# In the fourth layer of a graph network: half the pair-adds in every other chunk, the normalized rows in a buffer of their own, and GAT outputs and last operations two slots later

## The chip, the core and the metric

The kernel runs on one core of a Trainium2 chip. A core has five engines that run their own instruction queues in order and meet only at semaphores: TensorE (PE in the profile; its weight loads are PEld), VectorE (DVE), ScalarE (ACT), GpSimd (POOL) and SyncE (SP). DMAs are issued from queues of SP, ACT and POOL. The metric is the time of one execution on the device in microseconds; lower is better.

## What is computed

Four graph layers on 8 batches of 2048 nodes with 128 features, one shared 0/1 adjacency matrix. About 16 of 2048 entries of a row are set. Layers 0 and 1 are masked attention blocks with 8 heads and a feed-forward part. Layers 2 and 3 are GAT layers, and the change concerns these:

```python
def _L3_gnn_ref(x, adj, W, a_src, a_dst, ln_gamma, ln_beta):
...
    h = x @ W
    s_i = h @ a_src
    s_j = h @ a_dst
    e = s_i[:, :, None] + s_j[:, None, :]
    e = jnp.where(e >= 0, e, NEG_SLOPE * e)
    e = jnp.where(adj[None, :, :] == 0, -jnp.inf, e)
    att = jax.nn.softmax(e, axis=-1)
    att = jnp.nan_to_num(att, nan=0.0)
    out = jnp.einsum('bij,bjd->bid', att, h)
    y = out + x
    mu = jnp.mean(y, axis=-1, keepdims=True)
    var = jnp.mean((y - mu) ** 2, axis=-1, keepdims=True)
    return ln_gamma * (y - mu) * jax.lax.rsqrt(var + LN_EPS) + ln_beta
```

## The kernel before

**Tiles and chunks.** Nodes are sorted by their number of neighbours and cut into 16 tiles of 128 nodes, one node to a partition. Tile t has CAPS[t] slots, from 30 in tile 0 down to 11 in tile 15: slot s of a partition holds the s-th neighbour of that node. In a GAT layer the slots of a tile are cut into chunks of 4 or 3 (75 chunks with 277 slots in a layer). A chunk variable `k` is the first slot of the chunk in its tile. For each slot one indirect DMA (`gather`, line 320, queue of POOL) brings the row of the neighbour from the table of the layer in DRAM: 8 batches x 128 features and 2 x 8 weights, 1040 float32, 128 rows at a time. Chunks land in six buffers `kv0` to `kv5` that are used in turn; the gathers of a chunk wait until TensorE has read the chunk six before.

**What a GAT chunk does** (`gat_chunk`, a generator whose four parts are emitted at different times):

- Part A, lines 753 to 759: VectorE works out the weights of the slots by small products and maxima. They go to the PSUM tile `pair`, and those of two batches to the SBUF tile `ws`.
- Part B, lines 765 to 770: VectorE multiplies the rows of six batches by their weights (128x3072 for four slots), ScalarE those of the other two (two ACTIVATEs of 128x128 per slot).
- Part C, lines 772 to 774: VectorE adds the upper slots of the chunk to the lower ones in place, so of 4 slots 2 are left (an add of 128x2048), and of 3 also 2 (128x1024).
- Part D, lines 778 to 784: TensorE multiplies what is left by the identity and so sums it in the PSUM accumulator `acc`, two matmuls of 128x512 for each slot that is left. `acc` has two buffers, one per tile in work.

**What a tile does at its end.** `sums` (line 463 to 470) makes the reciprocals of the sums of weights. `tail` (line 1138) lets some slots pass and then emits `outputs` (line 657): `o = acc * sums` on VectorE, the only reader of `acc`. Then `gat_tail` starts a slot later: TensorE adds the residual and the bias (`added`, lines 801 to 810, PSUM tiles `m`), ScalarE squares with a sum (`squares`, line 817), GpSimd takes the power -1/2 (line 844, tile `rs`; it stands in the same queue as the gathers), three slots pass, ScalarE scales (`scaled`, line 825). In layer 2 each half is then transposed, projected to the table row of layer 3, and put into the table by an indirect DMA of GpSimd (`put_rows`, line 502); in layer 3 three slots pass, VectorE multiplies by gamma and adds beta (lines 858 and 860), and an indirect DMA of GpSimd writes the result (line 862). In layer 3 squares, scaled rows and result are held in the tile `rows`, of which there is one buffer.

**The order of the work** is written out by hand. `layers` goes over the chunks of all layers. For chunk i of a GAT layer it emits, in this order: `fetch` (the gathers of chunks up to four ahead); part A of chunk i; a slot; part B of chunk i; a slot; parts C and D of chunk i-1; a slot. A slot advances every waiting generator by one step, first `threads` (there a `tail` counts its slots), then `tails` (there a `gat_tail` makes one step). So a chunk is three slots long. Layer 3's first gathers are emitted once tiles 0 to 12 of layer 2 are put; the first chunks of layer 3 are those of tiles 0 and 1, in the order of `ORDER[4]`, with gathers from `sorted_lists`.

Of the kernel before, what the change touches and what calls it, by code (L numbers as in the profile page):

```python
# [8 lines left out]
F32 = mybir.dt.float32  # L9
# [8 lines left out]
P = 128  # L18
B, N, D = 8, 2048, 128
NT = N // P  # L20
NH = 8
# [7 lines left out]
NB = 8  # L29
# [8 lines left out]
CAPS = [BASE + FOLD, 23, 21, 20, 19, 18, 18, 17, 16, 16, 15, 14, 14, 13, 12, 11]  # L38
# [44 lines left out]
def sparse_path(ctx: ExitStack, tc: tile.TileContext, ins: dict, out: bass.AP, flag: bass.AP):  # L83
# [10 lines left out]
    nc = tc.nc  # L94
    const = ctx.enter_context(tc.tile_pool(name="const", bufs=1))
    work = ctx.enter_context(tc.tile_pool(name="work", bufs=2))
# [6 lines left out]
    def misc():  # L103
        return pm.tile([P, 512], F32, tag="m", name="m")
# [221 lines left out]
    def transpose4(src):  # L326
        pt = misc()
        for j in range(4):
            nc.tensor.transpose(pt[:, j * P : (j + 1) * P], src[:, j, :], ident)  # L329
        return pt.rearrange("p (b c) -> p b c", c=P)  # L330
# [111 lines left out]
    def folded_sums(w, box):  # L442

        columns = w.shape[-1]
        ps = misc()[:, :columns]
        for i in range(FOLD):
            nc.tensor.matmul(ps, merge, w[:, i, :], start=i == 0, stop=i == FOLD - 1)
        box["folded"] = small.tile([P, columns], F32, tag="folded", name="folded", bufs=1)
        nc.scalar.copy(box["folded"], ps)
# [107 lines left out]
    def state_done(l, t, box):  # L557


        box["halves"] = box.get("halves", 0) + 1  # L560
        if box["halves"] == 2:
            if l < 3:
                nc.sync.dma_start(kept[t], box["x"].rearrange("p b n -> p (b n)"))
                put_rows(l + 1, t, box["rows"])
                put[l + 1] += 1
            state(l, t + 3)
# [95 lines left out]
    def rows_of(box):  # L662
        if "rows" not in box:
            box["rows"] = work.tile([P, NB * 2 * D], F32, tag="rows", name="rows", bufs=1)
        return box["rows"]
# [70 lines left out]
    def gat_chunk(l, c):  # L736
        box, t, k, ns = c["box"], c["t"], c["k"], c["ns"]
        mine = own[:, t, :]
        if c["folded"]:
            pf = misc()[:, :NB]  # L740
            nc.tensor.matmul(pf, spread, mine, start=True, stop=True)
            mine = small.tile([P, NB], F32, tag="mine", name="mine", bufs=1)
            nc.scalar.copy(mine, pf)
            yield
        if k == 0:
            box["acc"] = pacc.tile([P, NB // 4, 512], F32, tag="acc", name="acc")
            at, n = (0 if t % 2 == 0 else 512 - NB * CAPS[t]), CAPS[t]
            box["w"] = pair[:, at : at + NB * n].rearrange("p (s b) -> p s b", b=NB)
        acc, w = box["acc"], box["w"]
        hs = c["buf"]  # L750
        wc = w[:, k : k + ns, :]
        wa, wb = hs[:, :, NB * D : NB * (D + 1)], hs[:, :, NB * (D + 1) :]
        nc.vector.tensor_mul(wb, wb, mine[:, None, :].to_broadcast([P, ns, NB]))
        nc.vector.tensor_max(wc, wa, wb)
        if c["folded"]:
            box["wf"] = small.tile([P, FOLD, NB], F32, tag="wf", name="wf", bufs=1)
            nc.vector.tensor_max(box["wf"], wa, wb)
        ws = small.tile([P, 4, SCALED], F32, tag="ws", name="ws", bufs=3)
        nc.vector.tensor_max(  # L759
            ws[:, :ns, :], wa[:, :, NB - SCALED :], wb[:, :, NB - SCALED :]  # L760
        )
        yield
        hv = hs[:, :, : NB * D].rearrange("p s (b c) -> p s b c", b=NB)
        nv = NB - SCALED
        nc.vector.tensor_mul(  # L765
            hv[:, :, :nv, :], hv[:, :, :nv, :], wc[:, :, :nv, None].to_broadcast([P, ns, nv, D])
        )
        for i in range(ns):
            for b in range(nv, NB):
                nc.scalar.mul(hv[:, i, b, :], hv[:, i, b, :], ws[:, i, b - nv : b - nv + 1])  # L770
        yield
        left = -(-ns // 2)
        if ns > 1:
            nc.vector.tensor_add(hv[:, : ns - left], hv[:, : ns - left], hv[:, left:ns])  # L774
        yield
        if c["folded"]:
            folded_sums(box["wf"], box)
        for i in range(left):
            for j in range(NB // 4):
                nc.tensor.matmul(  # L780
                    acc[:, j, :], merge if c["folded"] else ident, hv[:, i, 4 * j : 4 * j + 4, :],
                    start=k + i == 0, stop=c["last"] and i == left - 1,
                )
        yield

    def gat_tail(l, t, box):

        wt = W[l]
        xT = box["x"]
        if l == 2:  # L790
            ns = [work.tile([P, 4, D], F32, tag="n", name="n2") for _ in range(2)]
        else:
            n = rows_of(box)[:, : B * D].rearrange("p (b d) -> p b d", d=D)
            ns = [n[:, :4, :], n[:, 4:, :]]
        ys = [None, None]
        ss = small.tile([P, 8], F32, tag="ss", name="ss", bufs=3)
        rs = small.tile([P, 8], F32, tag="rs", name="rs", bufs=3)

        def added(h):
            ys[h] = y = misc().rearrange("p (b c) -> p b c", c=D)  # L800
            nc.tensor.matmul(
                y, ones_bf, wt["row_z"][:, None, :].to_broadcast([P, 4, D]),
                start=True, stop=False, skip_group_check=True,
            )
            nc.tensor.matmul(
                y, ident, box["o"][:, 4 * h : 4 * h + 4, :], start=False, stop=False,
                skip_group_check=True,
            )
            for j in range(4):
                nc.tensor.matmul(  # L810
                    y[:, j, :], xT[:, 4 * h + j, :], wt["res1"], start=False, stop=True,
                    skip_group_check=True,
                )

        def squares(h):
            for j in range(4):
                nc.scalar.activation(
                    ns[h][:, j, :], ys[h][:, j, :], AF.Square, bias=eps, scale=D**-0.5,
                    accum_out=ss[:, 4 * h + j : 4 * h + j + 1],
                )  # L820

        def scaled(h):
            for j in range(4):
                at = 4 * h + j
                nc.scalar.mul(ns[h][:, j, :], ys[h][:, j, :], rs[:, at : at + 1])  # L825

        def half_rows(h):
            scaled(h)
            yield
            pt = transpose4(ns[h])  # L830
            yield
            nc.scalar.copy(xT[:, 4 * h : 4 * h + 4, :], pt)
            yield
            yield from project(3, 4 * h, xT, rows_of(box), t)
            yield
            state_done(l, t, box)

        added(0)
        yield
        squares(0)  # L840
        added(1)
        yield
        squares(1)
        nc.gpsimd.tensor_tensor(rs, ss, half, op=ALU.pow)
        for _ in range(3):
            yield
        if l == 2:
            parts = [half_rows(0), later(2, lambda: half_rows(1))]
            while parts:
                advance(parts)  # L850
                yield
        else:
            scaled(0)
            yield
            scaled(1)
            for _ in range(3):
                yield
            nc.vector.tensor_mul(n, n, last_g[:, None, :].to_broadcast([P, B, D]))
            yield
            nc.vector.tensor_add(n, n, last_b[:, None, :].to_broadcast([P, B, D]))  # L860
            yield
            nc.gpsimd.indirect_dma_start(
                out=out, out_offset=bass.IndirectOffsetOnAxis(ap=perm[:, t : t + 1], axis=0),
                in_=n.rearrange("p b d -> p (b d)"), in_offset=None,
            )
            state_done(l, t, box)
            state_done(l, t, box)
# [213 lines left out]
    for l in range(4):  # L1081
        per = 2 if l < 2 else 4
        for t, k, ns, folded in pieces(l, per):
            c = dict(l=l, t=t, k=k, ns=ns, folded=folded, box=blocks[l][t])
# [48 lines left out]
    def later(n, make):  # L1133
        for _ in range(n):
            yield
        yield from make()

    def tail(l, t, box):
        for _ in range(2 if l < 2 else 3):
            yield  # L1140
        outputs(l, t, box)
        if l < 2:
            tails.append(later(1, lambda: attention_tail(l, t, box, 0)))
            tails.append(later(4, lambda: attention_tail(l, t, box, 4)))
        else:
            tails.append(later(1, lambda: gat_tail(l, t, box)))
        yield
# [600 lines left out]
```

## Time and profile before

| | us |
|---|---|
| median of 3 runs | 3423.61 (3417.87 to 3426.96) |
| the profiled execution | 3428.05 |
| its span | 3426.3 |
| layers 0 and 1, about | 353 to 2224 of the span |
| layer 2, steady part | 2360 to 2760 |
| from layer 2 to layer 3 | 2760 to 2890 |
| layer 3, from the last put to the last gather | 2890 to 3370 |
| end | 3370 to 3427 |

In the lines below, "busy" is the time in which an engine worked on an instruction; "x" is a count; "idle before us" is how long the engine stood still just before instructions of the group, and after the arrow stands what ended most of that. In a table of windows the columns are the stretch, its length, and for each engine its busy time with the number of instructions, then the granted clock of TensorE as a share of full speed, the mean busy share of the 16 DMA engines and the rate. A timeline line gives start, length, engine, line, operation, output and input.

### The profile page before, as it was taken

The numbers are of one execution on the slowest core, as the hardware profiler recorded it, in microseconds if no ns is written. First come the engines' busy times: TensorE is split into PE (matmuls) and PEld (weight loads), VectorE is DVE, ScalarE is ACT, GpSimd is POOL, SyncE is SP. The second block draws the span as 40 slices with busy tenths as digits, with TensorE's granted clock in tenths as the row PEclk, the third lists the DMA queues.
The fourth block names the chain that finished last, engine by engine and source line by source line (L and its number), as shares of the span: only waits on it lengthen the run. The fifth ranks groups of instructions, "written<-read, shape, count | busy, mean of one in ns | idle before, by whom it ended". The sixth has DMA issues, their size and how long they took to land.

```text
span 3426.3 us, 34767 instructions
## 1 busy us (share of the span) xinstructions
PE 2761.3 (81%) x10618; PEld 1595.4 (47%) x10618; DVE 3051.6 (89%) x2807; ACT 1425.1 (42%) x4972; POOL 2229.1 (65%) x1453
## 2 busy tenths in 40 slices
PE   5657888788899996888889899976888986767775
PEld 4523445455555652545455555553444543333332
DVE  8799999999999989999999999947867866889885
ACT  4712333334344441333334344453545654445444
POOL 0065888687667654566677666637767865788773
PEclk9888999999999999999999999998988998888887
DMA  8697778888878777677888888658988986899873
GB/s 326 201 355 275 284 283 303 307 303 301 312 290 296 277 287 280 238 309 284 335 298 292 315 297 295 241 171 307 326 290 311 352 326 214 291 313 334 304 275 118
DMA packets 200625, 986.52 MB, mean 288 GB/s; under 512 B 31918, under 2 KB 33712, under 8 KB 128436
## 3 DMA queue, kind: packets, MB, share of 16 engines
q0 software_dynamic: 175024, 890.45, 72.2%
q1 hardware_dynamic: 20502, 75.52, 5.9%
q10 hardware_dynamic: 4904, 18.24, 1.7%
q8 instruction: 87, 1.43, 0.2%
q14 instruction: 108, 0.88, 0.1%
HBM read 937.16 MB, written 91.55 MB: 300 GB/s over the span
## 4 chain that ended last, share of the span: by engine, by line
DVE 36%; PE 23%; issue 19%; DMA 11%; POOL 4%; ACT 4%; POOLq 0%; ACTq 0%; DVEq 0%; another core or an unknown queue 0%
DVE kv L614 13%; DVE kv L628 13%; PE acc L780 7%; PE acc L638 5%; DMA kv<-table,lists 4%; POOL kv L320 3%; DVE sc L617 3%; DMA kv<-table,sorted_lists 2%; DVE kv L774 2%; PE m L329 2%; DVE kv L765 2%; DMA table<-rows,perm 1%; DMA xs<-in_x_nodes_dram,perm 1%; PE m L720 1%; DVE w L459 1%
## 5 line engine op out<-in xcount | busy, mean ns | idle before, releaser
L320 POOL DMA_INDIRECT kv<-table,lists x955 | 1463.0, 1532 | 381.6 <-issue 203.6
L638 PE MATMUL acc<-kv,ident 128*128 128x512 f32 x2200 | 1109.0, 634 | 221.8 <-DVE kv L628 221.3
L780 PE MATMUL acc<-kv,ident 128*128 128x512 f32 x1184 | 622.2, 679 | 190.9 <-DVE kv L774 157.7
L638 PEld LDWEIGHTS acc<-kv,ident 128*128 128x128 f32 x2200 | 413.1, 201 | 652.7 <-issue 365.9
L617 DVE TENSOR_REDUCE sc<-kv 128x128 f32<-128x2048 f32 (+1 forms) x284 | 634.0, 2233 | 9.2
L628 DVE TENSOR_TENSOR kv<-kv,w 128x2048 f32<-128x2048 f32 (+1 forms) x284 | 631.5, 2223 | 8.6 <-ACT w L623 7.9
L614 DVE TENSOR_TENSOR kv<-kv,q 128x2048 f32<-128x2048 f32 (+1 forms) x282 | 629.2, 2231 | 10.7 <-DMA kv<-table,sorted_lists 5.7
L780 PEld LDWEIGHTS acc<-kv,ident 128*128 128x128 f32 x1184 | 248.9, 220 | 514.4 <-issue 294.8
L765 DVE TENSOR_TENSOR kv<-kv,pair 128x3072 f32<-128x3072 f32 (+1 forms) x150 | 466.2, 3108 | 1.0
L484 POOL TENSOR_TENSOR rs<-ss,half 128x4 f32<-128x4 f32 x128 | 222.8, 1741 | 313.9 <-ACT n L479 313.0
L774 DVE TENSOR_TENSOR kv<-kv 128x2048 f32<-128x2048 f32 (+1 forms) x150 | 296.1, 1974 | 145.9 <-ACT kv L770 137.0
L770 ACT ACTIVATE kv<-kv,ws 128x128 f32<-128x128 f32 x1108 | 339.0, 406 | 175.2 <-DVE ws L759 108.9
L479 ACT ACTIVATE n<-m,eps 128x128 f32<-128x128 f32 x512 | 181.0, 366 | 423.6 <-PE m L720 212.5
L623 ACT ACTIVATE w<-sc,lmask 128x64 f32<-128x64 f32 x554 | 165.1, 352 | 443.8 <-DVE sc L617 425.5
L320 POOL DMA_INDIRECT kv<-table,sorted_lists x153 | 203.5, 1330 | 114.8 <-PE acc L638 45.9
L488 ACT ACTIVATE n<-m,rs 128x128 f32<-128x128 f32 x512 | 146.0, 370 | 124.4 <-POOL rs L484 124.2
L502 POOL DMA_INDIRECT table<-rows,perm x57 | 102.5, 1798 | 129.1 <-ACT rows L553 33.2
L329 PE MATMUL m<-ident,n 128*128 128x128 f32 x640 | 105.2, 287 | 67.3 <-ACT n L825 47.4
L720 PE MATMUL m<-w_L_w,hT 128*128 128x128 f32 x1024 | 156.6, 275 | 1.7 <-ACT hT L704 1.7
L329 PEld LDWEIGHTS m<-ident,n 128*128 128x128 f32 x640 | 82.4, 147 | 132.6 <-ACT n L825 57.6
L720 PEld LDWEIGHTS m<-w_L_w,hT 128*128 128x128 f32 x1024 | 135.2, 192 | 1.9 <-ACT hT L704 1.9
L699 PE MATMUL m<-n1T,w_L_gnn_W 128*128 128x512 f32 x256 | 131.6, 597 | 0.8 <-ACT n1T L694 0.4
(242 smaller groups left out, 3476.4 us busy)
## 6 DMA issues: line engine op xcount, KB each, us to landing
kept<-xT SPq DMA_DIRECT2D x48, 512.0 KB
xT<-kept SPq DMA_DIRECT2D x48, 512.0 KB
kv<-in_adj_dram SPq DMA_DIRECT2D x16, 1024.0 KB
table<-kv ACTq DMA_DIRECT2D x16, 1024.0 KB
kv<-table,lists POOLq DMA_INDIRECT x955
kv<-in_x_nodes_dram SPq DMA_DIRECT2D x16, 512.0 KB
kv<-table,sorted_lists POOLq DMA_INDIRECT x153
found<-cand POOLq DMA_DIRECT2D x16, 64.0 KB
```

What stands on the lines that cost most here:

```text
L320: nc.gpsimd.indirect_dma_start(out=dst, out_offset=None, in_=tables[l][:, :], in_offset=bass.IndirectOffsetOnAxis(ap=index, axis=0), bound ...
L329: nc.tensor.transpose(pt[:, j * P : (j + 1) * P], src[:, j, :], ident)
L484: nc.gpsimd.tensor_tensor(rs, ss, half[:, :4], op=ALU.pow)
L614: nc.vector.tensor_mul(kk, kk, q[:, None].to_broadcast([P, ns, NB, D]))
L617: nc.vector.tensor_reduce(sc[:, :ns].rearrange("p s (b h) -> p (s b) h", h=NH), kk.rearrange("p s b (h j) -> p (s b) h j", h=NH), axis=AX. ...
L628: nc.vector.tensor_mul(vv, vv, w[:, k : k + ns, :].rearrange("p s (b h) -> p (s b) h", h=NH)[:, :, None, :] .to_broadcast([P, ns * NB, HD, ...
L638: nc.tensor.matmul(acc[:, j, :], merge if c["folded"] else ident, kv[:, i, 4 * j : 4 * j + 4, D:], start=k + i == 0, stop=c["last"] and i ...
L720: nc.tensor.matmul(y[:, j, :], hT[:, f, j, :], wt["2"][:, f, :], start=False, stop=f == 1, skip_group_check=True,)
L765: nc.vector.tensor_mul(hv[:, :, :nv, :], hv[:, :, :nv, :], wc[:, :, :nv, None].to_broadcast([P, ns, nv, D]))
L770: nc.scalar.mul(hv[:, i, b, :], hv[:, i, b, :], ws[:, i, b - nv : b - nv + 1])
L774: nc.vector.tensor_add(hv[:, : ns - left], hv[:, : ns - left], hv[:, left:ns])
L780: nc.tensor.matmul(acc[:, j, :], merge if c["folded"] else ident, hv[:, i, 4 * j : 4 * j + 4, :], start=k + i == 0, stop=c["last"] and i = ...
```

## The change

Three edits in the GAT layers:

1. In layer 3, chunks with `k % 8 == 0` add at most one pair. Where such a chunk has four slots, part C becomes an add of 128x1024 in place of 128x2048, three slots are left in place of two, and part D is six matmuls in place of four. That holds for 31 of the 75 chunks. Chunks of three or two slots stay as they are.
2. In layer 3 the tile for squares, scaled rows and result (`n` in `gat_tail`) is no longer a part of `rows` (one buffer) but a tile of the tag `w`, which has two buffers and has had no other use since layer 1.
3. `tail` lets five slots pass in place of three before `outputs`, for tiles 0 to 12 of layers 2 and 3; tiles 13 to 15 keep three. And in layer 3 five slots pass in place of three between `scaled` and the multiply by gamma, in all tiles. So the last operations of tiles 0 to 12 come four slots later in all.

```diff
@@ gat_chunk
         yield
-        left = -(-ns // 2)
-        if ns > 1:
-            nc.vector.tensor_add(hv[:, : ns - left], hv[:, : ns - left], hv[:, left:ns])
+
+        pairs = min(ns // 2, 1) if l == 3 and k % 8 == 0 else ns // 2
+        left = ns - pairs
+        if pairs > 0:
+            nc.vector.tensor_add(hv[:, :pairs], hv[:, :pairs], hv[:, left:ns])
         yield
@@ gat_tail
         else:
-            n = rows_of(box)[:, : B * D].rearrange("p (b d) -> p b d", d=D)
+            n = work.tile([P, max(CAPS), NB * NH], F32, tag="w", name="n")
+            n = n.rearrange("p s c -> p (s c)")[:, : B * D].rearrange("p (b d) -> p b d", d=D)
             ns = [n[:, :4, :], n[:, 4:, :]]
@@ gat_tail
             scaled(1)
-            for _ in range(3):
+            for _ in range(5):
                 yield
             nc.vector.tensor_mul(n, n, last_g[:, None, :].to_broadcast([P, B, D]))
@@ tail
     def tail(l, t, box):
-        for _ in range(2 if l < 2 else 3):
+        for _ in range(2 if l < 2 else 3 if t > NT - 4 else 5):
             yield
         outputs(l, t, box)
```

## The prediction, made before the result was known

> **What bounds the kernel now.** I read the page first, then a table of windows by stage, then the groups of GpSimd and VectorE within layer 3, then the waits and timelines there. Only GAT layers are touched, so 0 to 2224 us of the span stay as they are.
>
> ```profile
> core 0: us, PE busy (x) PEld busy (x) DVE busy (x) ACT busy (x) POOL busy (x), PEclk, DMA share, GB/s
> 2360.00:2760.00 400.00, 346.94 (x1260) 197.03 (x1259) 323.75 (x350) 214.77 (x842) 294.62 (x232) 0.90 0.91 320
> 2760.00:2890.00 130.00, 94.95 (x361) 54.83 (x359) 77.30 (x73) 61.72 (x245) 70.36 (x53) 0.86 0.69 243
> 2890.00:3370.00 480.00, 338.42 (x830) 153.81 (x831) 408.24 (x436) 207.31 (x789) 370.39 (x272) 0.85 0.88 304
> 3370.00:3427.00 57.00, 24.91 (x77) 12.99 (x75) 23.85 (x35) 21.45 (x94) 9.34 (x6) 0.76 0.08 31
> ```
>
> In layer 3 (third row) VectorE is busy 408 of 480 us, TensorE 338. GpSimd's 370 looks like slack and is not. Its groups and those of VectorE between 2925 and 3370 (445 us):
>
> ```profile
> L320 POOL DMA_INDIRECT kv<-table,lists x224 | 303.5, 1355 | 66.8 <-issue 46.6 <-PE acc L780 6.9 <-DMA kv<-table,lists 6.4
> L844 POOL TENSOR_TENSOR rs<-ss,half 128x8 f32<-128x8 f32 x13 | 22.2, 1709 | 28.2 <-ACT rows L817 28.1
> L862 POOL DMA_INDIRECT out_dram<-rows,perm x13 | 15.2, 1171 | 4.0 <-issue 4.0
> ```
>
> ```profile
> L774 DVE TENSOR_TENSOR kv<-kv 128x2048 f32<-128x2048 f32 x42 | 96.0, 2285 | 4.6 <-ACT kv L770 4.6
> L774 DVE TENSOR_TENSOR kv<-kv 128x1024 f32<-128x1024 f32 x20 | 24.5, 1223 | 29.4 <-ACT kv L770 29.4
> L858 DVE TENSOR_TENSOR rows<-rows,last_g 128x1024 f32<-128x1024 f32 x13 | 15.9, 1225 | 22.4 <-ACT rows L825 22.4
> ```
>
> Each gather has 0.30 us of issue ahead of it (66.8 / 224), so GpSimd accounts for 303.5 + 66.8 + 22.2 + 28.2 + 15.2 + 4.0 = 440 of 445 us: it never really waits for a free buffer, and its only idle time is 28 us ahead of the power L844. The queue that issues the gathers is full. VectorE has some 56 us of waits, for ScalarE (4.6 + 29.4 + 22.4). Where do these come from?
>
> ```profile
> ACT rows L817 <- DMA out_dram<-rows,perm: 80.3, 9, 15.8
> ACT rows L825 <- POOL rs L844: 49.4, 7, 12.9
> DVE kv L774 <- ACT kv L770: 34.0, 6, 9.3
> POOL rs L844 <- ACT rows L817: 28.1, 6, 8.4
> ```
>
> This is the list of waits in the same stretch. ScalarE's squares wait 80 us for the result DMA of the tile before, since both use the one buffer `rows`. One case, in the timelines of the three engines:
>
> ```profile
> 2968.24 1.01 POOL L862 DMA_INDIRECT out_dram<-rows,perm  x1 [0.30 <-issue]
> 2977.64 1.67 POOL L844 TENSOR_TENSOR rs<-ss,half 128x8 f32<-128x8 f32 x1 [8.39 <-ACT rows L817]
> ```
>
> ```profile
> 2974.59 0.37 ACT L817 ACTIVATE rows<-m,eps 128x128 f32<-128x128 f32 x1 [15.85 <-DMA out_dram<-rows,perm]
> ```
>
> ```profile
> 2979.25 1.22 DVE L774 TENSOR_TENSOR kv<-kv 128x1024 f32<-128x1024 f32 x1 [9.26 <-ACT kv L770]
> ```
>
> The result DMA is issued behind gathers at 2968.2, lands at 2974.6; ScalarE has stood for 15.9 us by then, with the chunk's products queued behind; so the add on VectorE waits 9.3 us; the power waits 8.4 us, and the gathers behind it with it. The DMA engines fell to 91 GB/s between 2970 and 2980.
>
> **What the Trainium skill says.** *SBUF — State Buffer*, "SBUF: two separate sides": VectorE and GpSimd share a port pair under an exclusive lock, which a VectorE instruction with two SBUF inputs takes against a GpSimd instruction that reads SBUF. The trace agrees: a gather takes 1.00 us alone, and up to 3.0 us where it meets the full add L774 (at 3105.55 it lasts 2.94, the add ends 2.08 after its start). The multiply L765, whose weights lie in PSUM, lengthens none. I gave each gather's time over 1.0 us between 2890 and 3370 to the add or gamma/beta operation it overlaps most: 45 full adds cost GpSimd 68.4 us, 1.52 each; 21 half adds 8.8 us, 0.42 each. *VectorE: DVE Perf Modes*, the section on the errata, prices a float32 add at (N+151)/0.96 ns: 2291 for 2048, 1224 for 1024; the trace has 2285 and 1223. *SBUF — State Buffer*, "A bandwidth-pool intuition that's wrong", gives HBM about 358 GB/s per core. Layer 3 moves 304; its best 50 us (2900 to 2950) show 337 at a busy share of 0.96, layer 2's best 358.
>
> **The change, part by part.**
>
> *Half adds.* Of the 31 chunks 4 lie before 2890 and 1 after 3370, so 26 in the window. VectorE: 26 x (2285 - 1223) = 27.6 us less. GpSimd: 26 x (1.52 - 0.42) = 28.6 us less. TensorE: 26 x 2 = 52 matmuls more at 0.68 us (mean of L780 over both GAT layers on the page) = 35 us, 338 to 374 of what is left of 480; they lie beside VectorE's work, as TensorE waits for L774 in that stretch (100 us in the list of waits), and a chunk's buffer comes free no later, since the add ends 1.06 us sooner and two matmuls take 1.3. If that cover were gone, TensorE's sum would still lie below the others.
>
> *`n` in two buffers.* The squares of tile t now wait for the result of tile t-2, issued about a tile (32 us) before: the 80.3 us on ScalarE go. With them the 28 us on GpSimd ahead of the power; I keep 5 for squares that are late for other reasons, so 23. VectorE's 34 us at L774 go too, but for what the power's place behind gathers still costs: L825's wait of 49.4 us stays, the power being emitted between the same two bursts of gathers as before. I keep 10.
>
> *Last operations two slots later.* VectorE's 22.4 us at L858 go: the multiply now comes after the next chunk's L765 (3.35 us), and the longest of these waits was 4.3. The result DMA is issued up to four slots (some 9 us) later; a tile's length of slack hides that. These two operations still lock GpSimd out (10 us in the window, both kernels).
>
> *Outputs two slots later.* In layer 3 `outputs` waited 1.1 us: nothing. In layer 2 the list of waits (2360 to 2760) gives o L657 <- PE acc L780 26.6 us in 7 waits of 0.3 to 5.7. Two slots put part A and B of a chunk ahead of it (0.55 + 3.35 = 3.9 us), so about 20 of the 26.6 go. But TensorE, which it waited for, is busy 347 of 400 there, and the DMA at 0.91; VectorE only runs into the next wait. Bounds -20 and +3; I take -6. Behind `outputs` on VectorE stand the chunks' operations; the accumulator it frees is wanted a tile later (at least 9 slots, used 6).
>
> *From layer 2 to layer 3.* The put of tile 12 (at 2786.89) is what layer 3's first gathers wait for (7.9 us on GpSimd, to 2797.29). Two slots later in the order costs two thirds of a chunk, about 4.5 us. Against that, the power of tile 13 (2802.23), now stuck behind those gathers, should come ahead of them: ScalarE waits 13.3 us for it, VectorE then 11.1. Bounds -8 and +6; I take 0.
>
> *The end.* Tile 15's squares waited for tile 14's result DMA (3407.45), though their inputs were done at 3405.3 and the first half's earlier: some 3 us. VectorE's wait of 4.0 us at 3376.7 has the same cause; 1 us is given back to two extra matmuls. I take -5.
>
> *Sum for layer 3.* GpSimd's floor: 480 - 28.6 - 23 = 428. VectorE's: 408 - 28 + 10 kept + 12 of waits for gathers at 2890 to 2925 and after = 402. TensorE's: 374. DMA: 304 x 480 = 146 MB, at 337 GB/s 433 us, at 358 408 us; at 325, the mean of the unbroken stretch 3050 to 3200 (share 0.94), 449 us. So GpSimd and the DMA engines become the limit together, and neither will run at its floor with the other's jitter. I take 444, which is -36, and keep 426 and 465 as ends.
>
> Total: -36 - 5 - 6 + 0 = -47. The profiled execution took 3428.05 (span 3426.3 and 1.75 around it), 4.4 us above the median of the runs shown, so 3381 on its own scale and 3377 on the median's; I give **3380**.
>
> **Rivals.** (1) *Likeliest*, as above: 3380, own range 3362 to 3398. (2) *The DMA engines are the bound already.* In the unbroken stretch they are busy 0.94 with stalls elsewhere refilled from buffers; then layer 3 gains only 15 us (465), layer 2 nothing, and the time is 3412. For it: the share. Against it: 10 us windows reach 366 to 391 GB/s. (3) *GpSimd's floor is reached* and VectorE's waits in layer 2 and at the transition pay in full: -54 - 8 - 20 = -82, 3344. (4) *Slower:* in layer 2 the moved tails bring the power one burst of gathers later. A burst is 4 x (1.355 + 0.3) = 6.6 us, on top of today's mean wait of 5.0 us (55.2 in 11 waits of L825 for L844 there); ScalarE has about one chunk, 6.6 us, between a product and its add, so 5.0 us of stall per tile for 13 tiles, +65, less 41 of layer 3 and the end: +24, 3452. It decides from 9 tiles of 13. For it: the case at 2802. Against it: by the order of slots, the power moves from the third slot of a chunk to the second, with no burst in between. That the second buffer does nothing is excluded: nothing else uses `w` in layer 3.
>
> **How the numbers follow.** Chances: likeliest 0.62, (2) 0.17, (3) 0.13, (4) 0.08. A measurement of this kernel can tell about 0.3%, here 10 us, from no change. Faster by more: 0.62 + 0.13 + half of (2), 0.08 = 0.83; within: the other half, 0.09; slower: 0.08. The range 3345 to 3414 leaves out (4), a quarter of (2) and about half of (3).
>
> **What would show it.** L817's wait for the result DMA gone; L858's and most of L774's waits gone; gathers' mean in layer 3 down from 1355 to about 1240 ns; GpSimd then waiting for `acc` (free buffers) or the DMA share at 0.93 or more; 26 adds turned from 2285 to 1223 ns; layer 3 some 36 us shorter. It is wrong if TensorE's `acc` releases hold the gathers, if the DMA rate stays near 305 GB/s without stalls, or if layer 2 grows.

## The result, and the profile after

The changed kernel takes 3337.15 us (median of 4 runs, 3326.53 to 3340.58), the kernel before beside it 3421.38 (4 runs): a ratio of 0.9752, 95% interval 0.9734 to 0.977. That is 84 us; the prediction said 47, and 3337 lies below its range, at about the time of its third rival. The profiled execution took 3326.53 (span 3324.7), 10.6 us under its median, while that of before lies 6.7 above its own; so the two traces differ by 101.6 us. From chip to chip the median of the kernel before was 3393 to 3421 us, so each run below is compared with the kernel before on its own chip. Traces of different chips are compared below as well; how far such traces scatter is told under e9.

The same table of windows as before (VectorE is the third engine column, GpSimd the fifth), cut at the same events:

```profile
2355.00:2754.00 399.00, 349.21 (x1332) 199.02 (x1333) 340.86 (x370) 228.16 (x900) 318.61 (x246) 0.94 0.95 345
2754.00:2841.00 87.00, 64.19 (x271) 38.37 (x270) 49.38 (x48) 41.18 (x167) 41.26 (x34) 0.86 0.67 238
2841.00:3270.00 429.00, 362.26 (x959) 167.27 (x958) 381.75 (x437) 213.81 (x827) 334.91 (x275) 0.94 0.94 339
3270.00:3325.00 55.00, 30.18 (x89) 15.27 (x87) 27.99 (x40) 19.30 (x80) 10.05 (x8) 0.80 0.18 70
```

Layer 3 moves 339 GB/s in place of 304 and is 429 us long. To compare many traces I cut each at four events into three stretches: the first GAT product on VectorE (L765), layer 2's last put (L502), the last gather (L320), the end of the span. Between them, in us:

| | first product to last put | last put to last gather | last gather to end |
|---|---|---|---|
| before | 655.1 | 484.7 | 62.8 |
| changed | 622.9 | 428.5 | 54.7 |
| difference | -32.2 | -56.2 | -8.1 |

The rest of the 101.6, 5.1 us, lies ahead of the first product, in code that is the same in both. The first stretch is layer 2 with the change to layer 3, the second layer 3, the third the end.

GpSimd's groups in the changed kernel between 2880 and 3270, and the adds and gamma products of VectorE there:

```profile
L320 POOL DMA_INDIRECT kv<-table,lists x224 | 271.5, 1212 | 67.9 <-issue 46.2 <-PE acc L782 9.2 <-DMA kv<-table,lists 5.4
L847 POOL TENSOR_TENSOR rs<-ss,half 128x8 f32<-128x8 f32 x13 | 22.4, 1727 | 7.3 <-ACT n L820 7.1
L865 POOL DMA_INDIRECT out_dram<-n,perm x12 | 15.0, 1247 | 3.7 <-issue 3.4 <-DVE kv L765 0.3
```

```profile
L776 DVE TENSOR_TENSOR kv<-kv 128x1024 f32<-128x1024 f32 x44 | 53.7, 1219 | 18.5 <-ACT kv L770 14.8 <-issue 3.8
L776 DVE TENSOR_TENSOR kv<-kv 128x2048 f32<-128x2048 f32 x17 | 38.9, 2286 | 8.1 <-ACT kv L770 5.3 <-issue 2.8
L861 DVE TENSOR_TENSOR n<-n,last_g 128x1024 f32<-128x1024 f32 x13 | 15.8, 1218 | 1.8 <-ACT n L828 1.8
```

The gathers' mean fell from 1355 to 1212 ns, the power's wait from 28.2 to 7.3 us, and the 224 gathers take 32 us less. GpSimd is still full: 271.5 + 67.9 + 22.4 + 7.3 + 15.0 + 3.7 = 388 of 390 us, and the few gathers from `sorted_lists` besides. VectorE's wait at the gamma product is down from 22.4 to 1.8 us.

In layer 2 (before 2360 to 2787, changed 2355 to 2754) the wait at `outputs` is gone. First before, then changed:

```profile
L657 DVE TENSOR_TENSOR o<-acc,sums 128x1024 f32<-128x1024 f32 x14 | 17.1, 1221 | 26.6 <-PE acc L780 26.6
```

```profile
L657 DVE TENSOR_TENSOR o<-acc,sums 128x1024 f32<-128x1024 f32 x14 | 17.0, 1218 | 0.0
```

And with it, in the lists of waits, GpSimd's own wait for buffers, which was this before and is 3.7 us in the changed kernel:

```profile
POOL kv L320 <- PE acc L780: 33.2, 20, 9.8
```

From layer 2 to layer 3 the power of tile 13 now stands ahead of the first gathers of layer 3, as the prediction said (GpSimd's timeline):

```profile
2754.14 1.02 POOL L502 DMA_INDIRECT table<-rows,perm  x1 [1.53 <-ACT rows L553]
2759.30 1.67 POOL L847 TENSOR_TENSOR rs<-ss,half 128x8 f32<-128x8 f32 x1 [4.14 <-ACT n L820]
2761.16 1.06 POOL L320 DMA_INDIRECT kv<-table,sorted_lists  x1 [0.19 <-PE acc L782]
```

The stretch from tile 12's put to tile 15's went from 91.9 to 87.3 us, of which 4.6 are in the -32.2 above.

### The profile page after: what moved, and what is told of

It is laid out like the page before. It is cut to its first block, busy times and chain, and to the rows that moved or that the text cites. A ratio compares the mean times of both kernels' runs of the same rounds, so it can differ in the third digit from the quotient of the medians.

```text
span 3324.7 us, 35030 instructions
## 1 busy us (share of the span) xinstructions
PE 2759.3 (83%) x10742; PEld 1594.5 (48%) x10742; DVE 3018.8 (91%) x2807; ACT 1424.0 (43%) x4972; POOL 2191.1 (66%) x1453
## 4 chain that ended last, share of the span: by engine, by line
DVE 39%; issue 21%; PE 20%; DMA 8%; POOL 5%; ACT 4%; POOLq 0%; DVEq 0%; another core or an unknown queue 0%; ACTq 0%
DVE kv L628 14%; DVE kv L614 14%; PE acc L782 6%; PE acc L638 5%; POOL kv L320 3%; DMA kv<-table,lists 3%; DMA kv<-table,sorted_lists 3%; DVE sc L617 3%; DVE kv L765 2%; DVE kv L776 2%; PE m L720 1%; PE m L329 1%; DVE w L459 1%; DMA table<-rows,perm 1%; PE m L520 1%
## 5 line engine op out<-in xcount | busy, mean ns | idle before, releaser
L320 POOL DMA_INDIRECT kv<-table,lists x955 | 1439.0, 1507 | 346.5 <-issue 203.6
L765 DVE TENSOR_TENSOR kv<-kv,pair 128x3072 f32<-128x3072 f32 (+1 forms) x150 | 466.3, 3108 | 1.8
L776 DVE TENSOR_TENSOR kv<-kv 128x2048 f32<-128x2048 f32 (+1 forms) x150 | 263.1, 1754 | 128.2 <-ACT kv L770 101.7
L479 ACT ACTIVATE n<-m,eps 128x128 f32<-128x128 f32 x512 | 181.4, 367 | 424.4 <-PE m L720 215.3
L320 POOL DMA_INDIRECT kv<-table,sorted_lists x153 | 198.2, 1295 | 106.2 <-PE acc L638 46.4
L820 ACT ACTIVATE n<-m,eps 128x128 f32<-128x128 f32 x256 | 90.4, 368 | 245.5 <-PE m L813 110.1
L502 POOL DMA_INDIRECT table<-rows,perm x57 | 94.4, 1656 | 129.8 <-ACT rows L553 36.0
```

What stands on the lines that cost most here:

```text
L320: nc.gpsimd.indirect_dma_start(out=dst, out_offset=None, in_=tables[l][:, :], in_offset=bass.IndirectOffsetOnAxis(ap=index, axis=0), bound ...
L765: nc.vector.tensor_mul(hv[:, :, :nv, :], hv[:, :, :nv, :], wc[:, :, :nv, None].to_broadcast([P, ns, nv, D]))
L776: nc.vector.tensor_add(hv[:, :pairs], hv[:, :pairs], hv[:, left:ns])
```

## The experiments

My theory after the result: layer 3 runs at the pace of GpSimd's full queue, whose load fell to just the floor that the prediction had worked out and then not believed; layer 2 got back what the wait at `outputs` had held up (this second half of the theory did not hold, see e13). Rivals: layer 3 is paced by VectorE, or by the DMA engines, or by TensorE; layer 2's gain is another thing than that wait.

### One part alone, or one part undone

**e1: outputs later in layer 2 alone.** The kernel before with

```diff
-        for _ in range(2 if l < 2 else 3):
+        for _ in range(2 if l < 2 else 3 if t > NT - 4 or l == 3 else 5):
```

> The kernel before with one edit: outputs two slots later in layer 2 alone (tiles 0 to 12). Theory (the wait of VectorE for acc was what held layer 2 back, and with it GpSimd's gathers): layer 2 is 25 to 30 us shorter, layer 3 as before; about 3393. Rival (as I predicted: VectorE runs into the next wait, TensorE being busy 0.87): 6 us, about 3415.

Measured: 3393.21 against 3415.27, ratio 0.9943 (0.9924 to 0.9962), 22 us less. The stretches are 623.5, 483.9 and 62.2: all of it is in layer 2, 31.6 us by this trace against that of before, which was made on another chip.

**e3: outputs as before, all else changed.**

```diff
-        for _ in range(2 if l < 2 else 3 if t > NT - 4 else 5):
+        for _ in range(2 if l < 2 else 3):
```

> The changed kernel with outputs after three slots again in layers 2 and 3; the other edits kept. Theory (the later outputs pay in layer 2 alone): layer 2 loses 25 to 30 us, layer 3 nothing, about 3365. Rival (in layer 3, with TensorE busier by 52 matmuls, VectorE now waits for acc too, 1 to 2 us a tile): 15 to 25 us more, about 3385.

Measured: 3347.11, ratio 0.9793 (0.9773 to 0.9812) to before, so the later outputs are worth about 0.4% here, some 14 us: less than e1 gave, and less than the 25 to 30 expected. The trace, of the slowest of the four executions, has 649.8, 425.6 and 54.8: layer 3 is as short as in the changed kernel without them. They pay in layer 2 alone; the rival falls.

**e4: the second buffer alone.** The kernel before with

```diff
-            n = rows_of(box)[:, : B * D].rearrange("p (b d) -> p b d", d=D)
+            n = work.tile([P, max(CAPS), NB * NH], F32, tag="w", name="n")
+            n = n.rearrange("p s c -> p (s c)")[:, : B * D].rearrange("p (b d) -> p b d", d=D)
```

> The kernel before with n in a tile of its own with two buffers, nothing else. Theory (GpSimd's queue loses 28 us at the power, which waits for squares that wait for the result DMA; 23 of them come back, and 3 to 5 at the end): about 3394. Rival (VectorE's 22 us at the multiply by gamma stay and take the place): 8 us or less, about 3414.

Measured: 3374.13 against 3415.27, ratio 0.9876 (0.9854 to 0.9898): 41 us, the largest of the parts. The stretches: 644.9, 452.7, 53.9, so layer 3 is 32.0 us shorter and the end 8.9. GpSimd's groups (2900 to 3318) and, from the list of waits, VectorE's wait at the gamma product:

```profile
L320 POOL DMA_INDIRECT kv<-table,lists x223 | 290.7, 1303 | 66.5 <-issue 42.2 <-PE acc L782 8.4 <-DMA kv<-table,lists 6.4
L847 POOL TENSOR_TENSOR rs<-ss,half 128x8 f32<-128x8 f32 x13 | 25.7, 1980 | 1.4 <-ACT n L820 1.1
```

```profile
DVE n L861 <- ACT n L828: 23.8, 10, 3.6
```

The power's wait fell from 28.2 to 1.4 us; VectorE's 23.8 us at the gamma product stayed and took nothing away. So the rival falls, and the gain is 18 us larger than the theory had it: the gathers got shorter too (1303 ns in the mean for 1355), which I had not expected and have not traced further.

**e2: all edits but the half adds.**

```diff
-        pairs = min(ns // 2, 1) if l == 3 and k % 8 == 0 else ns // 2
+        pairs = ns // 2
```

> The changed kernel with all pair-adds whole again. Theory (layer 3 runs at the pace of GpSimd's full queue, and an add of half size frees it by 1.1 us): layer 3 is 28 us longer, about 3365. Rival (the DMA engines set the pace of the changed kernel, at 339 GB/s and 0.94): GpSimd has slack to give, 5 to 10 us, about 3345.

Measured: 3356.81, ratio 0.9826 (0.9808 to 0.9843), against 0.9752 for the whole change, so the half adds are worth about 0.7%, some 25 us by the two ratios. The stretches: 630.9, 451.0, 54.6. Against e4's 452.7 the later last operations, which take VectorE's 23.8 us away, give 1.7 us, no more than traces differ by. The half adds give 451.0 - 428.5 = 22.5, near the 28 expected; the rival's 5 to 10 us fall.

The reverse of e4, the changed kernel with one buffer, has no run.

### What paces layer 3

**e5: VectorE's time given back, without the lock.** The lock is the hold on the shared port pair that the prediction names. The changed kernel with this ahead of the add:

```diff
+        if l == 3 and k % 8 == 0 and ns == 4:
+            junk = small.tile([P, 3], F32, tag="sink", name="sink", bufs=1)
+            nc.vector.tensor_reduce(
+                junk, W[1]["qkv"][:, :315][:, None, :].to_broadcast([P, 3, 315]), axis=AX.X, op=ALU.add
+            )
```

> The changed kernel with a VectorE reduction of a constant tile (128x945 float32 to 128x3, one SBUF input, about 1.1 us, result unused) ahead of the add in each of the 31 changed chunks: it gives VectorE back the time that the half adds saved, but not the hold on the shared port. Theory (the half adds pay through GpSimd's queue): 0 to 6 us more than the changed kernel. Rival (they pay through VectorE's own time): 20 to 25 us more, as much as whole adds cost.

Measured: 3331.65 against 3392.86, ratio 0.9811 (0.9786 to 0.9836). The changed kernel itself has no run on that chip. The nearest is e6 below, 3318.89 there with 3.6 us of small additions, and e5 is 12.8 us above it: more than the theory's 6, less than the rival's 20. The trace shows where. The 31 reductions took 1.13 us each, 26 of them in layer 3 with 29 us in all; VectorE is as busy there (406 us) as in the kernel before (408), and the stretches are 622.2, 428.4 and 58.9:

```profile
2843.00:3271.00 428.00, 358.35 (x952) 165.43 (x951) 406.00 (x455) 211.55 (x813) 338.14 (x274) 0.94 0.95 340
```

Layer 3 is 0.1 us shorter than in the trace of the changed kernel, 4.4 longer than e6's 424.0 and 7.1 longer than the 421.3 of e9 below; the end is 5.7 longer than e6's. So 29 us of VectorE's time in layer 3 came back there as 7 us at most. The gathers' mean stayed at 1208 ns, where it was 1355 with VectorE equally busy in whole adds. VectorE's time is a small part of what the half adds give; most of it goes through the gathers.

**e6 and e10: GpSimd's queue made longer.** In the same place, on GpSimd, in e6 a memset alone (of 0.0), in e10 with the power:

```diff
+        if l == 3 and k % 8 == 0 and ns == 4:
+            junk = small.tile([P, 4], F32, tag="sink", name="sink", bufs=1)
+            nc.gpsimd.memset(junk, 1.0)
+            nc.gpsimd.tensor_tensor(junk, junk, half[:, :4], op=ALU.pow)
```

> The changed kernel with one small memset on GpSimd (128x4, unused) in each of the 31 changed chunks. Theory (GpSimd's queue is full and sets the pace in layer 3): all of the memsets' time with their gaps comes back in layer 3, 31 times about 0.5 to 1.3 us, 15 to 40 us. Rival (the DMA engines or TensorE set the pace of the changed kernel): 0 to 8 us.

Measured: 3318.89, ratio 0.978 (0.9754 to 0.9806); layer 3 at 424.0. The memsets took 0.115 us each, 3.6 us in all: too small a probe to tell.

> The changed kernel with a memset (128x4) and a power (128x4) on GpSimd in each of the 31 changed chunks, results unused, about 1.9 us together; 26 of them in layer 3's stretch. Theory (GpSimd's full queue sets the pace of layer 3): 26 x 1.9 = 49 us more there, less what now falls into its waits: 40 to 50 us more than the changed kernel. Rival (the DMA engines or TensorE set the pace): 0 to 15 us more.

Measured: 3359.38, beside the changed kernel at 3337.15 on the same chip (**e9** below). The trace shows memset and power at 0.11 and 1.14 us, not the 1.9 that I had taken, so 26 of them are 33 us. The median rose by 22, and layer 3 is 459.3 us against 428.5 and 421.3 in the two traces of the changed kernel, 31 to 38 more. GpSimd is full again (2880 to 3295):

```profile
L320 POOL DMA_INDIRECT kv<-table,lists x223 | 277.3, 1243 | 64.6 <-issue 45.1 <-PE acc L786 13.0 <-ACT kv L770 1.8
L776 POOL TENSOR_TENSOR sink<-sink,half 128x4 f32<-128x4 f32 x24 | 27.4, 1142 | 2.0
```

The median's 22 us lie beyond the rival's 15 and below the theory's 40. Against the 33 us that were really added, two thirds come back by the medians and all of it by the traces of layer 3.

> The changed kernel itself again, as the measure for the others on this chip. Expected: about 0.975 of the kernel before, with layer 3 (last put to last gather) at 425 to 430 us in the trace.

Measured: 0.977 (0.9756 to 0.9784) of before, stretches 631.8, 421.3 and 55.9; layer 3 is just below the 425 to 430 expected. This is the scatter of single traces: layer 3 is 421.3 to 428.5 in those where it is coded as in the changed kernel and nothing is added (the changed kernel, e3, e7, e9). The first stretch scatters more, from 614.7 to 631.8 in ten traces in which layer 2 is coded alike. A difference of a few us between two traces means nothing.

**e8 and e12: more half adds, and no adds.**

```diff
-        pairs = min(ns // 2, 1) if l == 3 and k % 8 == 0 else ns // 2
+        pairs = min(ns // 2, 1) if l == 3 else ns // 2
```

> The changed kernel with half adds in all 53 four-slot chunks of layer 3, 22 more. Theory (GpSimd's queue): 22 x 1.1 = 24 us less there, of which the DMA engines, at 0.94 and 339 GB/s, allow about half: 10 us shorter. Rival (TensorE becomes the bound): 0 to 10 us longer.

Measured: 3301.53, ratio 0.9724 (0.9705 to 0.9743) to a kernel before of 3392.86; against e6 on its chip, which is nearly the changed kernel, 17 us less, where 10 were expected and the rival said longer. Layer 3 takes 409.2:

```profile
2837.00:3246.00 409.00, 381.45 (x1035) 178.97 (x1034) 361.82 (x436) 213.06 (x822) 323.51 (x275) 0.97 0.97 356
```

The DMA engines move 356 GB/s at 0.97: the 304 and 339 at which the kernel before and the changed one ran were what GpSimd asked for, no limit. And GpSimd is still full: gathers, powers and result DMAs with the idle time before them make up all of the 366 us from 2880 to 3246, with the gathers at 1162 ns. For e12 `pairs` is 0 in layer 3:

> The changed kernel with no pair-add at all in layer 3: TensorE sums all slots, 277 x 2 matmuls in place of 360. Theory (past the half adds TensorE is the next bound: 381 us busy of 409 with all half adds, and 75 x 2 matmuls of about 0.6 us come on top): layer 3 at about 470 us, 40 us longer than the changed kernel. Rival (GpSimd's queue still sets the pace): shorter by 10 to 20 us.

Measured: 3392.02, ratio 0.9927 (0.9908 to 0.9946); layer 3 468.9 us, as the theory had it. GpSimd's gathers are those from 2880 to 3315:

```profile
2846.00:3315.00 469.00, 469.00 (x1266) 222.07 (x1265) 279.36 (x356) 207.40 (x802) 286.52 (x275) 1.00 0.86 309
```

```profile
L320 POOL DMA_INDIRECT kv<-table,lists x224 | 227.5, 1016 | 98.8 <-PE acc L782 50.6 <-issue 40.0 <-PE m L813 4.8
```

TensorE is busy without a gap and is the bound. And with no adds the gathers take 1016 ns in the mean, close to the 1.00 of a gather alone, though GpSimd's work is the same. The load of the DMA engines can't be the reason, 309 GB/s here and 304 before: what stretched the gathers to 1355 was the adds. Now, too, GpSimd waits for buffers (50.6 us for `acc`), as it does where it isn't the bound.

**e7 and e11: layer 2 as well.** Half adds in every other chunk of layer 2 (e7: the condition `l == 3` left out), and with all chunks of layer 3 (e11: `l == 3 or k % 8 == 0`).

> The changed kernel with the half adds in layer 2 as well. Theory (layer 2 too now runs at the pace of GpSimd's queue): some 15 to 25 us shorter. Rival (TensorE, busy 0.88 there, takes 37 us of matmuls more and becomes the bound): 0 to 15 us longer.

Measured: 3311.12, ratio 0.9758 (0.9738 to 0.9777), 8 us less than e6 on that chip; TensorE is busy 390 of 405 us in layer 2. Between theory and rival: a small gain, with TensorE nearly full.

> The changed kernel with half adds in every other chunk of layer 2 and in all four-slot chunks of layer 3. Theory (two stages, each with its own gain, 14 us in layer 2 and 19 in layer 3 by the traces of the runs before): about 33 us less than the changed kernel. Rival (TensorE takes the gain back where both layers meet): 20 us or less.

Measured: 3303.39, ratio 0.9674 (0.9658 to 0.969), 34 us less than the changed kernel on that chip. It has the lowest ratio of all runs here.

### What layer 2's gain is

**e13: the tail later, outputs in place.** The kernel before with

```diff
-            tails.append(later(1, lambda: gat_tail(l, t, box)))
+            tails.append(later(3 if l == 2 and t <= NT - 4 else 1, lambda: gat_tail(l, t, box)))
```

> The kernel before with outputs where they were, but the start of the tail behind them (TensorE's residual, ScalarE's squares, the power on GpSimd, the put) two slots later in layer 2, tiles 0 to 12. Theory (layer 2's gain is VectorE's wait for acc at outputs, which this leaves as it was): 0 to 5 us. Rival (the gain is the tail's new place among gathers and chunks: TensorE's and GpSimd's tail work two slots later): 20 us or more less than before.

Measured: 3381.99 against 3394.55, ratio 0.9969 (0.996 to 0.9979): 12.6 us, more than the theory and less than the rival. In its trace the first stretch is 613.5 us, and from the list of waits:

```profile
DVE o L657 <- PE acc L782: 6.1, 4, 3.7
```

`outputs` stands where it stood, and its wait is down from 26.6 to 6.1; the first stretch is as short as with `outputs` moved. So the theory falls: the gain doesn't hang on where `outputs` stands. What moves in both edits is the tail behind it. The trace of before shows what the old place did (timelines of TensorE, GpSimd and VectorE):

```profile
2500.28 2.07 PE L535 MATMUL m<-w_L_h,xT 128*128 128x128 f32 x8 [4.73 <-ACT xT L832]
2507.95 1.00 POOL L320 DMA_INDIRECT kv<-table,lists  x1 [9.85 <-PE acc L780]
2510.11 1.22 DVE L657 TENSOR_TENSOR o<-acc,sums 128x1024 f32<-128x1024 f32 x1 [5.22 <-PE acc L780]
```

TensorE stands 4.7 us inside a tail, at the projection L535, until ScalarE has copied `xT`. The sums L780 that free buffers and complete `acc` are emitted behind it. The gather waits for them from 2498.1, VectorE at `outputs` only from 2504.9. So GpSimd's wait is no consequence of VectorE's: both wait for TensorE's sums. The other long waits of gathers for buffers in layer 2 begin 4 to 7 us ahead of the wait at `outputs` too. TensorE's idle time ahead of L535 (2360 to 2780) is 17 to 20 us in the four traces with the old order (before, e3, e4, e15), and 6.0 us in the changed kernel and in e13. That this idle time alone makes the gain no run isolates, and why ScalarE is late there stays open (VectorE's add, too, waits 9.5 us for it, until 2502.6).

**e14: one slot in place of two** (`else 4`, layer 2 alone).

> The kernel before with outputs one slot later in place of two, in layer 2 alone. That slot puts part A of the next chunk (0.55 us on VectorE) ahead of outputs, but not part B (3.35 us). Theory (what counts is the VectorE work ahead of the wait): 7 waits x 0.55 us, about 4 us less than before, against 22 for two slots. Rival (the place of the tail counts, and shifts by half): 8 to 15 us less.

Measured: 3396.13 against 3394.55, ratio 1.0008 (1.0001 to 1.0015): no gain, less than the theory's 4 us. But its trace looks like one with two slots: the first stretch is 625.6 us, the wait at `outputs` 9.6 us in place of 26.6, GpSimd's for buffers 9.8, TensorE's at L535 none. So either one slot clears most of the waits and something else takes the gain away, or on a chip where before takes 3395 layer 2 is short on its own.

**e15 and e16: before again, and e1 again, on one chip.**

> The kernel before itself, for a second trace. Theory (layer 2's 655 us from its first product to its last put belong to the kernel): 645 to 660 us again. Rival (the wait for acc in layer 2 depends on small differences in timing, and the profiled execution was a bad one): 625 to 640 us.

> The kernel before with outputs two slots later in layer 2 alone, beside the kernel before on the same chip. Theory: 22 us less, layer 2 at 615 to 625 us from first product to last put. Rival (as above): 10 us or less, since layer 2 of the kernel before is short on its own here.

Measured: e15 3415.58, stretches 648.2, 483.4 and 62.3; e16 3395.86, ratio 0.9937 (0.9914 to 0.9961) to before, stretches 624.1, 484.4 and 62.5. So layer 2's gain is the kernel's: 24 us here by the traces and 19 to 22 by the medians, and the four traces with the old order have 644.9 to 655.1 us in the first stretch, the ten with two slots more 614.7 to 631.8. The profiled execution of before was some 7 us longer in layer 2 than this one. On chips where before takes 3393 to 3395 the gain may be less; on one of them e6 is 74 us under before, 8 more than the 66 that e4 and the half adds give together on another chip. Why before is faster there stays open: there is no trace of before on such a chip.

## Why the prediction was right in direction and wrong in size

**Right.** The full queue of GpSimd was found in the profile, with the lock and the power's wait as its two avoidable loads; the power of tile 13 moved ahead of layer 3's first gathers; layer 3 has nothing of the later outputs; TensorE has room for 52 matmuls more; the squares' 80 us of waits for the result DMA are gone from the list of waits. GpSimd's floor of 428 us for layer 3 was met: 428.5 and 421.3. (The floor was worked out for 480 us of layer 3; on the scale of the events, 484.7, it is 433, so the load fell by 5 to 12 us more than the two items in it.)

**Wrong, step "Sum for layer 3".** I took 444 in place of 428, since the DMA engines at 325 to 337 GB/s and 0.94 to 0.96 seemed to be a bound at 433 to 449. That rate was the load: e8 moves 356 GB/s, close to the 358 that the Trainium skill states (*SBUF — State Buffer*, "A bandwidth-pool intuition that's wrong"), which I had quoted and then set aside for a mean of the trace. e8, whose GpSimd is still full, shows that the queue and not the rate held the kernel. The term is -56 where I took -36.

**Wrong in one term: the second buffer.** I kept 5 of the power's 28 us of wait; e4 leaves 1.4, and its gathers are shorter too (1303 for 1355 ns): 32 us in place of 23, by the two traces. The half adds gave 22.5 to 29.7 us (451.0 against 428.5 and 421.3), where I had 28.6.

**Wrong, step "Outputs two slots later".** I took -6, with -20 as the most, because TensorE was busy 0.87 and VectorE would run into its next wait. e1 and e16 gave 19 to 22 us by the medians and 24 to 32 by the traces. The step priced VectorE's wait at `outputs` alone and left out that the tail behind it moves as well. With the tail, TensorE's stand ahead of L535 falls from 19.7 to 6.0 us and GpSimd's wait for buffers from 33.2 to 3.7; e13, which moves the tail alone, clears the waits as well. TensorE's busy share of 0.87 didn't tell that its idle time stood just ahead of the sums that free the buffers.

**Without effect.** VectorE's 22.4 us at the gamma product, listed as a gain, were worth 1.7 (e2 against e4). The end gave 8.1 where I had 5. And one sentence doesn't add up: the add ends 1.06 us sooner and two matmuls take 1.3, so a chunk's buffer comes free some 0.3 us later, and not "no later"; GpSimd's wait for `acc` in layer 3 is 9.2 us where it was 6.9, so that cost little.

The three mis-sized terms make up the miss: 56, 19 to 22 and 8 are 83 to 86 us, against 84 measured. By the medians, e1's 22, e4's 41 and the half adds' 25 sum to 88: the parts add up too.

## What to carry to other kernels

An engine's busy share isn't its load: add the gap ahead of each instruction (0.30 us per gather here) before calling it idle, and look whether its waits are for free buffers (it has slack) or only for late inputs (it paces the rest). A transfer rate in a profile is a limit only where something else has been seen to push against it; until then it is the demand. And before pricing a wait, look for what it is a sign of: VectorE's 26.6 us in layer 2 and GpSimd's 33.2 were both waits for TensorE's sums, behind its stand in the tail of another tile, and went together, while 22.4 us on VectorE in layer 3 held up nothing. When an edit moves one operation, list what moves with it.

## What the runs showed of the hardware

In the kernel before, an add of 128x2048 float32 with both inputs in SBUF costs the gathers beside it 1.5 us of its 2.29, one of half the length 0.42 of 1.22: in both cases its length less about 0.8 us, so halving an add saves more than half of the cost. Single gathers took up to 3.1 us. Without the adds the gathers take 1016 ns in the mean. A power of 128x4 on GpSimd took 1.14 us in e10, right behind a memset, and 1.7 for 128x8 elsewhere. The same program took 3393 to 3421 us on different chips (medians), which is more than most of the edits here are worth.
